# Graph attention on one core: VectorE multiplies two heads, not one, in six steps of 32 instead of two

## The chip, the core and the metric

The kernel runs on one core of a Trainium2 chip. Five engines work beside each other, each with its own queue of instructions: TensorE (PE, with its weight loads listed apart as PEld), VectorE (DVE), ScalarE (ACT), GpSimd (POOL) and SyncE (SP, which here only issues DMAs). They wait for one another through semaphores. The metric is the device time of one execution in microseconds; the time of the kernel before is the median of three runs.

## The reference

Two layers over 4096 nodes of 512 features, with one dense 4096 x 4096 matrix `adj` that is both the edge weight and the mask. Layer 0 is a single-head attention with `adj` added twice to the logits. The change touches layer 1 alone, a graph attention with 8 heads of 64 features:

```python
h = jnp.maximum(_layernorm(x, axis=-1), 0.0)
nX = (h @ W).reshape(n, NHEAD, OUT_DIM).transpose(1, 0, 2)
nX = a_ln * (nX - mean) / (std + EPS) + b_ln           # per head
at1 = jnp.einsum('kno,ok->kn', nX, a1)[:, :, None]
at2 = jnp.einsum('kno,ok->kn', nX, a2)[:, :, None]
kg = leaky_relu(at1 + at2.transpose(0, 2, 1), 0.2)     # head x node x node
kg = kg * graph[None]
mg = jnp.where(mask[None], kg, NEG_FILL)
attention = jax.nn.softmax(mg, axis=-1)
y = attention @ nX + nX
x = x + jax.nn.elu(y.transpose(1, 0, 2).reshape(n, 512))
```

So for each of 8 heads and each pair of nodes a logit is formed, multiplied by the edge weight, exponentiated and used as weight in a sum over nodes.

## The kernel before

`fast_path` does the work (a second path for extreme values is compiled in and is not run here). Layer 0 takes the first 2070 us or so. Layer 1 runs in 512 steps: 8 chunks of 512 target nodes, in each chunk 2 groups of 4 heads (`HG`), and in each of these 16 groups 32 steps over blocks of 128 source nodes (`NB` = 32). "Group k" below is the k-th of these 16, and "step m of a group" the step with number m modulo 32. One step handles a block of 128 sources x 512 targets for four heads; its results go through these functions:

- `z_sums(n+1)`, TensorE: into two PSUM tiles `d`, each holding two heads (`pair[0]`: heads 0 and 1, `pair[1]`: heads 2 and 3), it puts the sum of the two attention terms (L950) and then the mask, as a product of a bf16 tile with an identity (L955). There are three such buffers for the two tiles of a step. The order is heads 2, 3, 0, 1.
- `relu(n+1)`, ScalarE: for heads 0 and 1 a Relu into the SBUF tile `t` (L962). Six buffers of `t` exist.
- `leaky(n)`, VectorE: for heads 2 and 3 one `scalar_tensor_tensor` each (L972), then the product with the edge weights `g` for as many heads as VectorE has to take (`mine`, L977), then the addition of `pair[0]` to heads 0 and 1 of `t` (L978), which completes their leaky ReLU.
- `weigh(n)`, GpSimd: the product with `g` for the remaining heads, all of them in SBUF (L985).
- `exponent(n-3)`, ScalarE: the exponent of all four heads, 2048 columns (L988).
- `values(n-4)`, TensorE: the product with the features `nX`, accumulated over the 32 steps (L1001).

Each engine takes its instructions in the order in which the loop emits them: within iteration n of the loop `values(n-4)`, `exponent(n-3)`, `leaky(n)`, `weigh(n)`, `z_sums(n+1)`, `relu(n+1)`. So ScalarE takes the Relu of step n+1 only after the exponent of step n-3, and TensorE starts the sums of step n+1 only after the value products of step n-4.

At the end of a group `finish` spreads further work over the first steps of the next one: ScalarE copies the accumulators in step 3 (L1017), TensorE turns them back to rows in steps 4 and 5 (L1023), VectorE divides and adds in the same steps (L1032 to L1035), ScalarE does the passes of the ELU in steps 7 to 11 (L1045 to L1055), and GpSimd two additions of 1024 columns in steps 12 and 13 (L1059, L1063). Group 0 also carries the layer norm, projection and split of the last chunk's rows (`make_ready`, L258 to L408), and groups 1 to 4 each carry two GpSimd passes over 512 columns for those rows (L349, L350, in the fifth step).

How many heads VectorE multiplies is decided by the set `light`: in a step of the set VectorE takes two heads (3 and 2) and GpSimd two; in all other steps VectorE takes one and GpSimd three. Where VectorE takes two, the second L972 leaves its result in PSUM (`pair[1]`) instead of writing it to `t`.

Of the kernel before, what the change touches and what calls it, by code (L numbers as in the profile page):

```python
# [23 lines left out]
NB = N // P  # L24
# [22 lines left out]
@with_exitstack  # L47
def adj_preln_gnn_kernel(
    ctx: ExitStack,
    tc: tile.TileContext,  # L50
    x: bass.AP,
    adj: bass.AP,
    wqT: bass.AP,
    bq: bass.AP,
    wkT: bass.AP,
    bk: bass.AP,
    wvT: bass.AP,
    bv: bass.AP,
    w1: bass.AP,
    a1T: bass.AP,  # L60
    a2T: bass.AP,
    a_ln: bass.AP,
    b_ln: bass.AP,
    out: bass.AP,
):
    nc = tc.nc
    keep = ctx.enter_context(tc.tile_pool(name="keep", bufs=1))
    flag = keep.tile([1, 1], mybir.dt.int32, name="flag")
    fast_path(
        tc, flag, x, adj, wqT, bq, wkT, bk, wvT, bv, w1, a1T, a2T, a_ln, b_ln, out  # L70
    )

    low = nc.values_load(flag[0:1, 0:1])  # L73
    with tc.If(low > 0):
        general_path(tc, x, adj, wqT, bq, wkT, bk, wvT, bv, w1, a1T, a2T, a_ln, b_ln, out)
# [3 lines left out]
def fast_path(  # L79
# [796 lines left out]
    with tc.tile_pool(name="ga_in", bufs=2) as inputs, tc.tile_pool(  # L876
# [6 lines left out]
        n_steps = len(STEPS)  # L883
# [1 line left out]
        inverses = gat.tile([P, NI, 2, 2, 2, 4], F32, name="inverses")  # L885
        loads, logits, zs, groups = {}, {}, {}, {}

        light = {n + d for n in range(NB + 3, n_steps, NB) for d in (9, 10)}
        later = {}

        def load_adj(q):
# [684 lines left out]
```

## Time and profile before

| | us |
|---|---|
| median of 3 runs | 3968.43 (3968.31 to 3969.87) |
| profiled execution | 3965.98 |
| its span, first to last instruction | 3964.2 |
| layer 1: first product on GpSimd (L985) starts | 2092.1 |
| last product on GpSimd starts | 3937.3 |
| group 0 (start of one group's first L985 to the next's) | 157.0 |
| groups 1 to 4, each | 114.6 to 114.7 |
| groups 5 to 14, each | 112.1 to 112.2 |

A line of the timeline reads: start, duration (both in us), engine, line of the kernel, operation, what is written and read with its shape, how many instructions are merged in it, and in brackets the idle time of the engine before it with the instruction that ended this. A line of the groups reads: line, engine, operation, shapes, count, then busy us and mean ns of one, then the idle time before it and what ended most of it. Two instructions of VectorE can overlap a little at their ends in these records, so the distance from start to start says more of its pace than the sum of durations. A line of the windows gives the window, its length, and the busy us of each engine in it, then the granted clock of TensorE (1.00 is full), the DMA engines' busy share and GB/s.

### The profile page before, as it was taken

What the parts mean: (1) busy time and instruction counts of PE and PEld (TensorE: products, weight loads), DVE (VectorE), ACT (ScalarE), POOL (GpSimd) and SP (SyncE); (2) the same over time, 40 slices, a digit from 0 to 9 for tenths busy, and PEclk for the clock granted to TensorE, in tenths of its full rate; (3) what the DMA queues carried; (4) which work ended last, traced back from release to release, by engine and by line L of the source; (5) the groups of instructions that cost most, each with busy time, mean ns of one, the idle gap of its engine ahead of it and who ended that gap; (6) DMA issues with size and microseconds to landing.
All of it is one profiled execution on the core that took longest, in us unless ns stands there. A gap on an engine that the chain in (4) does not pass through costs nothing. (4 is left out here: it accounts for less than half of the span.)

```text
span 3964.2 us, 43905 instructions
## 1 busy us (share of the span) xinstructions
PE 3774.4 (95%) x15217; PEld 1789.4 (45%) x15370; DVE 2890.3 (73%) x4328; ACT 1797.0 (45%) x1581; POOL 2564.4 (65%) x1281
## 2 busy tenths in 40 slices
PE   8989999999999999999998899999999999999997
PEld 4446666666666666666653222222222222222222
DVE  5435556565565656556556799999999999999996
ACT  1001011111111111111115688888888888888887
POOL 3432225243242525234256999999999999999998
PEclk9999999999999999999998999999999999999999
DMA  6466656667675766757556544444444444444442
GB/s 208 175 206 193 201 179 204 200 194 211 184 220 161 222 182 191 214 186 222 166 153 189 145 138 146 146 142 142 134 143 144 139 145 146 146 140 146 132 150 79
DMA packets 554407, 670.37 MB, mean 169 GB/s; under 512 B 79808, under 2 KB 397504, under 8 KB 534720
## 3 DMA queue, kind: packets, MB, share of 16 engines
q1 hardware_dynamic: 552112, 665.70, 54.7%
q8 instruction: 122, 2.00, 0.2%
q10 hardware_dynamic: 2064, 1.77, 0.2%
q14 instruction: 109, 0.89, 0.1%
HBM read 495.12 MB, written 172.23 MB: 168 GB/s over the span
## 5 line engine op out<-in xcount | busy, mean ns | idle before, releaser
L985 POOL TENSOR_TENSOR t<-t,g 128x1536 f32<-128x1536 f32 (+1 forms) x512 | 1724.0, 3440 | 47.6 <-DVE t L978 26.9
L1001 PE MATMUL acc<-t,nX 128*64 128x512 f32 x4096 | 996.3, 607 | 72.1 <-ACT t L988 58.0
L737 POOL TENSOR_TENSOR total<-total,aT 128x512 f32<-128x512 f32 x248 | 340.5, 1373 | 1059.0 <-ACT aT L732 1051.9
L988 ACT ACTIVATE t<-t 128x2048 f32<-128x2048 f32 x512 | 975.8, 1906 | 87.7 <-POOL t L985 86.6
L747 PE MATMUL acc<-v,aT 128*128 128x512 f32 x2048 | 961.9, 593 | 0.0
L732 ACT ACTIVATE aT<-aT 128x512 f32<-128x512 f32 x256 | 161.3, 630 | 1323.2 <-DVE aT L727 1315.2
L962 ACT ACTIVATE t<-d 128x1024 f32<-128x1024 f32 x512 | 524.8, 1025 | 239.1 <-PE d L955 216.6
L978 DVE TENSOR_TENSOR t<-t,d 128x1024 f32<-128x1024 f32 x512 | 620.2, 1211 | 7.3 <-ACT t L962 7.3
L955 PE MATMUL d<-nb,ident_b 128*128 128x512 bf16 x1895 | 514.8, 385 | 14.9 <-issue 9.3
L1001 PEld LDWEIGHTS acc<-t,nX 128*64 128x64 f32 x4096 | 250.5, 136 | 597.6 <-issue 340.9
L747 PEld LDWEIGHTS acc<-v,aT 128*128 128x128 f32 x2048 | 389.9, 190 | 272.3 <-issue 244.8
L972 DVE SCALAR_TENSOR_TENSOR d<-u,at2m,d 128x512 f32<-128x512 f32 x542 | 407.3, 752 | 51.9 <-PE d L955 31.1
L727 DVE TENSOR_TENSOR aT<-aT,X 128x256 f32<-128x256 f32 x512 | 215.0, 420 | 279.6 <-PE X L719 276.3
L972 DVE SCALAR_TENSOR_TENSOR t<-u,at2m,d 128x512 f32<-128x512 f32 x482 | 360.0, 747 | 50.0 <-DVE d L972 0.9
L727 DVE TENSOR_TENSOR aT<-aT,Z 128x256 f32<-128x256 f32 x384 | 159.6, 416 | 290.5 <-PE Z L719 285.8
L977 DVE TENSOR_TENSOR t<-d,g 128x512 f32<-128x512 f32 (+1 forms) x512 | 366.3, 715 | 4.3 <-DMA g<-gT_d 1.4
L950 PE MATMUL d<-z,z 6*128 6x512 bf16 x2048 | 252.2, 386 | 45.5 <-DVE t L977 22.7
L711 DVE SCALAR_TENSOR_TENSOR gs<-ng,aT 128x512 f32<-128x512 bf16 x256 | 286.0, 1117 | 10.3 <-DMA gT_d<-gs 1.7
L950 PEld LDWEIGHTS <-z 6*128 6x128 bf16 x2048 | 76.8, 91 | 456.0 <-issue 451.9
L719 PE MATMUL Z<-qt,hS 128*128 128x256 f32 x1024 | 266.0, 383 | 8.6 <-DVE aT L727 8.4
L955 PEld LDWEIGHTS <-ident_b 128*128 128x128 bf16 x2048 | 159.2, 98 | 242.9 <-issue 123.4
L719 PE MATMUL X<-qt,hS 128*128 128x256 f32 x1024 | 263.9, 381 | 0.0
(161 smaller groups left out, 3120.6 us busy)
## 6 DMA issues: line engine op xcount, KB each, us to landing
g<-gT_d SPq DMA_DIRECT2D x128, 1024.0 KB, 5.5
ag<-in_adj_dram SPq DMA_DIRECT2D x256, 256.0 KB, 5.2
hT<-h_d SPq DMA_DIRECT2D x64, 1024.0 KB, 5.9
hS<-s_d SPq DMA_DIRECT2D x64, 1024.0 KB, 8.2
gT_d<-gs SPq DMA_DIRECT2D x256, 256.0 KB, 2.7
nb<-nT_d SPq DMA_DIRECT2D x128, 512.0 KB, 5.3
nT_d<-ng SPq DMA_DIRECT2D x256, 128.0 KB, 3.1
z<-z_d SPq DMA_DIRECT2D x143, 128.0 KB, 4.7
```

Source lines behind the costliest of these rows:

```text
L719: seq(nc.tensor.matmul(out, a, b, start=start and k == 0, stop=k == 1, skip_group_check=not start,))
L727: seq(nc.vector.tensor_add(p, p, part))
L737: seq(nc.gpsimd.tensor_add(totals[ic], totals[ic], p))
L747: seq(nc.tensor.matmul(sums[ic][b], probs[s][:, ts(b, P)], v[:, jt, :], start=jt == 0, stop=jt == NB - 1))
L955: seq(nc.tensor.matmul(pair[hh // 2][:, hh % 2, :], ident_b, ng[:, jt % JB, :], start=False, stop=True))
L962: seq(nc.scalar.activation(t[:, 0:2, :], zs[n][0], AF.Relu, scale=4.0))
L972: seq(nc.vector.scalar_tensor_tensor(pair[1][:, e, :] if e > 1 - mine else t[:, 2, :], u4[:, e, :], at2m[:, jt, h : h + 1], pair[1][:, e, ...
L977: seq(nc.vector.tensor_mul(t[:, HG - mine : HG, :], pair[1][:, 2 - mine : 2, :], g))
L978: seq(nc.vector.tensor_add(t[:, 0:2, :], t[:, 0:2, :], pair[0]))
L985: seq(nc.gpsimd.tensor_mul(t[:, 0:mine, :], t[:, 0:mine, :], g))
L988: seq(nc.scalar.activation(logits[n], logits[n], AF.Exp))
L1001: seq(nc.tensor.matmul(grp["acc"][hf][ts(e, HD), :], nX[jt // SB][:, jt % SB, hg * HG + 2 * hf + e, :], t[:, 2 * hf + e, :], start=jt == 0 ...
```

## The change

The set `light` is replaced. Before, it held two steps in each of groups 1 to 15: steps 12 and 13, those in which GpSimd also has its two additions for the group before. Now it holds steps 1, 8, 12, 13, 19 and 25 of every group, group 0 included. Nothing else is edited, and no instruction changes its place in its queue; the shapes and operands of L972, L977 and L985 in the steps concerned follow from the set. (One blank line is added too, so in the changed kernel the lines below it have numbers higher by one.)

```diff
-        light = {n + d for n in range(NB + 3, n_steps, NB) for d in (9, 10)}
+
+        light = {n for n in range(n_steps) if n % NB in (1, 8, 12, 13, 19, 25)}
         later = {}
```

Where the set is used (unchanged):

```python
def leaky(n):
    ...
    mine = 2 if n in light else 1
    for e in (1, 0):
        h = hg * HG + 2 + e
        seq(nc.vector.scalar_tensor_tensor(
            pair[1][:, e, :] if e > 1 - mine else t[:, 2, :], u4[:, e, :],
            at2m[:, jt, h : h + 1], pair[1][:, e, :], ALU.max, ALU.add,
        ))
    g = loads[n // JB][0][:, jt % JB, :].unsqueeze(1).to_broadcast([P, mine, GC])
    seq(nc.vector.tensor_mul(t[:, HG - mine : HG, :], pair[1][:, 2 - mine : 2, :], g))
    seq(nc.vector.tensor_add(t[:, 0:2, :], t[:, 0:2, :], pair[0]))

def weigh(n):
    mine = 2 if n in light else 3
    g = loads[n // JB][0][:, STEPS[n][2] % JB, :].unsqueeze(1).to_broadcast([P, mine, GC])
    t = logits[n]
    seq(nc.gpsimd.tensor_mul(t[:, 0:mine, :], t[:, 0:mine, :], g))
```

## The prediction

> **What bounds the kernel now.** I read the page first (busy shares), then the busy time per window, the groups by line with shapes kept apart, the waits, and last the timeline of VectorE, because the change moves work between two engines that are both nearly full. The page, and the windows of three whole groups of 32 steps in layer 1:
>
> ```profile
> PE 3774.4 (95%) x15217; PEld 1789.4 (45%) x15370; DVE 2890.3 (73%) x4328; ACT 1797.0 (45%) x1581; POOL 2564.4 (65%) x1281
> ...
> 2363.72:2478.47 114.75, 106.50 (x523) 31.66 (x528) 106.92 (x135) 96.44 (x72) 114.67 (x38) 1.00 0.45 141
> 2707.71:2819.83 112.12, 106.09 (x520) 32.24 (x528) 105.97 (x135) 95.78 (x72) 112.12 (x35) 1.00 0.44 142
> 2819.83:2931.94 112.11, 106.22 (x521) 32.27 (x528) 106.00 (x135) 95.83 (x72) 112.11 (x35) 1.00 0.45 142
> ```
>
> The windows' columns after the length are PE, weight loads, DVE, ACT, POOL. From about 2090 us on, one group lasts 112.1 us (114.7 in groups 1 to 4) and GpSimd is busy for all of it: it sets the pace. VectorE shows 106, but this understates it, as the gap it needs between two instructions is not busy time. Its timeline, in the first group that GpSimd does not hold back, and the last step of layer 1:
>
> ```profile
> 2243.12 1.21 DVE L978 TENSOR_TENSOR t<-t,d 128x1024 f32<-128x1024 f32 x1
> ...
> 2286.26 1.22 DVE L978 TENSOR_TENSOR t<-t,d 128x1024 f32<-128x1024 f32 x1 [0.27 <-ACT t L962]
> 2288.20 1.55 DVE L972 SCALAR_TENSOR_TENSOR d<-u,at2m,d 128x512 f32<-128x512 f32 x2 [0.73 <-PE d L955]
> 2289.84 1.23 DVE L977 TENSOR_TENSOR t<-d,g 128x1024 f32<-128x1024 f32 x1
> 2290.99 1.21 DVE L978 TENSOR_TENSOR t<-t,d 128x1024 f32<-128x1024 f32 x1
> 2292.11 1.54 DVE L972 SCALAR_TENSOR_TENSOR d<-u,at2m,d 128x512 f32<-128x512 f32 x2
> 2293.76 1.23 DVE L977 TENSOR_TENSOR t<-d,g 128x1024 f32<-128x1024 f32 x1
> 2294.90 1.21 DVE L978 TENSOR_TENSOR t<-t,d 128x1024 f32<-128x1024 f32 x1
> 2296.03 0.75 DVE L972 SCALAR_TENSOR_TENSOR d<-u,at2m,d 128x512 f32<-128x512 f32 x1
> ...
> 2299.28 0.75 DVE L972 SCALAR_TENSOR_TENSOR d<-u,at2m,d 128x512 f32<-128x512 f32 x1
> ...
> 2353.67 1.21 DVE L978 TENSOR_TENSOR t<-t,d 128x1024 f32<-128x1024 f32 x1
> ...
> 3930.70 1.21 DVE L978 TENSOR_TENSOR t<-t,d 128x1024 f32<-128x1024 f32 x1
> ```
>
> A step with one head on VectorE takes 2299.28 - 2296.03 = 3.25 us from start to start, with no wait in it; a step with two ("light", because it is light for GpSimd) takes 2296.03 - 2292.11 = 3.92 us. The whole group from 2243.12 to 2353.67 takes 110.55 us; its last two steps were already held by GpSimd (0.14 and 0.18 us over 3.25), so VectorE alone needs 110.2 us for a group with two light steps. GpSimd's 112.1 stands only 1.9 us over it. That margin decides the case.
>
> GpSimd's own prices, by shape, and the order of a group around its two light steps:
>
> ```profile
> L985 POOL TENSOR_TENSOR t<-t,g 128x1536 f32<-128x1536 f32 x481 | 1649.3, 3504 | 27.0 <-DVE t L978 26.9
> L985 POOL TENSOR_TENSOR t<-t,g 128x1024 f32<-128x1024 f32 x30 | 72.4, 2412 | 0.0
> ...
> 2863.26 2.43 POOL L1059 TENSOR_TENSOR e<-e,y 128x1024 f32<-128x1024 f32 x1
> 2865.57 2.45 POOL L985 TENSOR_TENSOR t<-t,g 128x1024 f32<-128x1024 f32 x1
> 2867.90 2.46 POOL L1063 TENSOR_TENSOR e<-e,xi 128x1024 f32<-128x1024 f32 x1
> 2870.24 65.26 POOL L985 TENSOR_TENSOR t<-t,g 128x1536 f32<-128x1536 f32 x19
> ```
>
> From start to start a product of three heads costs 65.26/19 = 3.43 us, one of two heads or an ELU addition about 2.33 us: 30 x 3.43 + 4 x 2.33 = 112.2 us, the measured group. In groups 1 to 4 the two passes for the last chunk's own rows (L349, L350) add 2.55 us.
>
> [...] The rows of L977 show 1225 and 684[...] the trace has 3504 - 2412 = 1092 ns. So a head costs GpSimd about twice what it costs VectorE, and moving one looks like a bargain. [...] the light steps at 2288 to 2296 run with GpSimd busy and keep their prices. [...] VectorE has little time to give.
>
> **The change part by part.** The set goes from two light steps in each of groups 1 to 15 (12 and 13 modulo 32: 30 steps) to six in each of the 16 groups (1, 8, 12, 13, 19, 25: 96 steps). No queue is reordered and no DMA moves; in each of the 66 further steps L985 shrinks to 1024 columns, L977 grows to 1024, and the second result of L972 stays in PSUM.
>
> GpSimd: four more light steps a group save 4 x (3.43 - 2.33) = 4.4, so 107.8 us (110.3 in groups 1 to 4).
>
> VectorE: four more light steps add 4 x (3.92 - 3.25) = 2.7, so 112.9 us at most. The bound changes hands: GpSimd now idles about 5 us a group, which costs nothing, and absorbs the 2.55 us of groups 1 to 4.
>
> Can VectorE follow its own sum? In the group above its waits beyond the plain prices are 0.5 us before the reciprocal of step 4, and 0.2, 0.36 and 0.8 us in steps 10 to 12, where ScalarE's extra passes for ELU (steps 7 to 11) make its exponents late, PE's value products wait for those, and the sums of the next step come late. Step 8, now light, gives ScalarE and PE 0.67 us just before. Following the instructions: the 0.2 of step 10 goes (PE waited 0.24 us for the exponent there), but the two Relu passes and the Exp that make steps 11 and 12 late start about 0.5 us later too, so most of that stays. I take 0.15 us off: 112.75. Bounds: nothing comes off (112.9), or all 0.67 (112.2). For the other added steps I find no cover: steps 1, 19 and 25 lie where VectorE runs back to back.
>
> How long were the 15 groups before, by VectorE's own clock? (3930.70 - 2243.12)/15 = 112.5 us; the 114.7 of groups 1 to 4 and the 112.1 of the rest, less the ground VectorE had to give up at first. So 15 x (112.75 - 112.5) = +3.8 us.
>
> The end: GpSimd now trails VectorE by 5.44 us at the last step (VectorE's last addition ends at 3931.9, GpSimd's last product starts at 3937.3), and the tail hangs on GpSimd. With VectorE as pacer the backlog is built afresh in each group: from nothing at step 12, +0.74 at 13 (2.33 + 2.33 - 3.92), +1.4 at 14, +0.18 in each plain step, and -0.48 and then -0.9 around each of steps 19 and 25, which leaves about 1.8 at step 31. That gives -3.6 us.
>
> Group 0 (2092 to 2249 us) has no light step now and gets six. Steps 8 and 12 are hidden: VectorE then waits more than 3 us for the projection's matmuls anyway (L301 waits on PE). Step 25 is on the path, step 1 and 13 too (the next sums wait for L977). Step 19 adds 0.67 on VectorE but takes 1.1 from GpSimd ahead of the scalars' split, which PE waits for. Between +1.2 and +2.7; I take +2.0.
>
> Sum: +3.8 - 3.6 + 2.0 = +2.2 us. The profiled execution took 3965.98 us (span 3964.2 and 1.8 around it), so it would take 3968.2; the median shown is 3968.43, 2.5 above, and I carry the difference to it: 3970.6, say 3970.5.
>
> **Rivals.**
> 1. ScalarE's lateness in steps 10 to 12 dissolves, with VectorE and GpSimd no longer entangled. Then 1.37 us of wait go in each group: 110.2 + 2.7 - 1.37 = 111.5, 15 x (111.5 - 112.5) - 3.6 + 2.0 = -17, or 3952 us. For it: step 8 is light just there. Against: the same waits stand, to 0.01 us, in groups where GpSimd's backlog differs by 2.6 us, so they do not come from GpSimd but from ScalarE's own sum, which is the same after.
> 2. Slower, by one mechanism: PE has almost no slack. A plain PE round takes about 3.24 us against VectorE's 3.25, and half of the next step's sums cannot start before L977 has released its PSUM pair. L977 is 0.55 us longer in a light step, so the first L972 after each added light step may wait, as it waits 0.54 us in step 1 at 2092 us where PE's clock is low. 60 added steps x 0.54 = 32 us, 4002 us. Against: after both light steps at 2288 and 2292 L972 starts with no wait. It decides from (7.9 - 2.2)/60 = 0.1 us per added step.
> 3. GpSimd's saving arrives whole (15 x 4.4 = 66 us, 3902): would need VectorE at 107.8 a group, which its own 110.2 with only two light steps excludes. No chance given.
>
> **How the numbers follow.** A measurement of this kernel tells about 0.2% (7.9 us) from no change. My forecast, that the pace passes to VectorE at nearly the same value, has 0.77: its bounds (15 x -0.55 and 15 x +0.15, and 0.2 us of unforeseen wait a group upward, the group 0 spread) give 3961 to 3977, nearly all within 0.2%; of it 0.70 no change, 0.06 slower, 0.01 faster. Rival 1 has 0.09 (0.08 faster, 0.01 no change), rival 2 0.14, all slower, with smaller waits likelier than the full one. Faster 0.09, no change 0.71, slower 0.20. The range 3961 to 3980 leaves out rival 1 and most of rival 2.
>
> **What would show it.** GpSimd's busy time in a group window falls to about 108 of about 112.7, with idle before L985 released by L978; VectorE's step is 3.92 in six places and 3.25 elsewhere; groups 1 to 4 become 2 us shorter and the later ones 0.6 us longer. L972 idle on PE after plain light steps would show rival 2; no waits at steps 10 to 12, rival 1. A group under 111.5 or over 113.3 us would make the forecast wrong.

## The result, and the profile after

| | before | after |
|---|---|---|
| median of 12 runs | 3968.26 us (3965.82 to 3970.69) | 3968.94 us (3965.39 to 3971.58) |
| after / before | | 1.0002 (95%: 0.9994 to 1.0009) |
| profiled span | 3964.2 us | 3968.8 us |
| of it from the start of the first L985 (L986 after) to the end | 1872.07 us | 1871.95 us |

The change moves the time by nothing that can be measured. The 4.6 us between the two profiled spans lie ahead of GpSimd's first product of layer 1, where nothing was changed: it starts at 2092.1 us in one execution and at 2096.9 in the other. From there to the end the two need the same.

That is a sum of parts that cancel, not a change without effect. First the busy time of the engines on the page after, then three whole groups of 32 steps (groups 2, 5 and 6; after the length: PE, weight loads, DVE, ACT, POOL), then GpSimd's waits from group 1 on (who waits, for whom, us, times, longest). All line numbers after are higher by one.

```profile
PE 3810.7 (96%) x15370; PEld 1800.1 (45%) x15370; DVE 2918.1 (74%) x4328; ACT 1783.0 (45%) x1581; POOL 2495.9 (63%) x1281
```

```profile
2361.27:2474.28 113.01, 108.57 (x531) 33.08 (x530) 107.73 (x135) 94.71 (x73) 110.37 (x37) 1.00 0.46 143
2699.88:2812.53 112.65, 108.56 (x530) 33.06 (x528) 107.72 (x135) 94.98 (x73) 108.01 (x35) 1.00 0.45 142
2812.53:2925.18 112.65, 108.56 (x530) 33.06 (x528) 107.72 (x135) 94.98 (x73) 107.97 (x35) 1.00 0.45 142
```

```profile
POOL t L986 <- DVE t L979: 62.0, 67, 1.4
```

GpSimd's 112.1 us of work a group have become 108.0, and the 4.6 that it lacks to 112.65 are idle time, ended by VectorE's last instruction of a step (62 us in all, 4.1 a group, in the line above). Before, GpSimd waited for nothing from group 1 on. VectorE is the pacer now, although its 107.7 busy us are 96% of the window. The busy share does not tell it: the engine that sets the pace is busy for 107.7 us of a group, and one with 4.6 us to spare for 108.0. A reader has to go to the timeline. VectorE's, around a light step away from all waits (step 19 of group 6):

```profile
2880.83 1.21 DVE L979 TENSOR_TENSOR t<-t,d 128x1024 f32<-128x1024 f32 x1
2881.96 1.54 DVE L973 SCALAR_TENSOR_TENSOR d<-u,at2m,d 128x512 f32<-128x512 f32 x2
2883.60 1.23 DVE L978 TENSOR_TENSOR t<-d,g 128x1024 f32<-128x1024 f32 x1
2884.74 1.21 DVE L979 TENSOR_TENSOR t<-t,d 128x1024 f32<-128x1024 f32 x1
2885.87 0.75 DVE L973 SCALAR_TENSOR_TENSOR d<-u,at2m,d 128x512 f32<-128x512 f32 x1
2886.73 0.75 DVE L973 SCALAR_TENSOR_TENSOR t<-u,at2m,d 128x512 f32<-128x512 f32 x1
2887.39 0.68 DVE L978 TENSOR_TENSOR t<-d,g 128x512 f32<-128x512 f32 x1
2887.99 1.21 DVE L979 TENSOR_TENSOR t<-t,d 128x1024 f32<-128x1024 f32 x1
```

The light step takes 2885.87 - 2881.96 = 3.91 us, and the step behind it has no idle time in brackets: each instruction follows the one before at the usual distance, 0.1 us behind the end of an L973 that leaves its result in PSUM (`d`), and 0.08 or 0.09 us before the end of any other. There are 38 such L973 in a group, so some 3.8 us: most of the 4.9 that the busy sum leaves out.

The rest of the sum reads off VectorE's last addition of group 0 and of group 15, and off GpSimd's last product, after and before:

```profile
2248.12 1.21 DVE L979 TENSOR_TENSOR t<-t,d 128x1024 f32<-128x1024 f32 x1
...
3938.93 1.21 DVE L979 TENSOR_TENSOR t<-t,d 128x1024 f32<-128x1024 f32 x1
```

```profile
3941.90 3.50 POOL L986 TENSOR_TENSOR t<-t,g 128x1536 f32<-128x1536 f32 x1
...
3937.33 3.49 POOL L985 TENSOR_TENSOR t<-t,g 128x1536 f32<-128x1536 f32 x1
```

(3938.93 - 2248.12)/15 = 112.72 us a group, against 112.51 before: +3.2 us over 15 groups. GpSimd's last product starts 2.97 us behind the start of VectorE's last addition (6.63 before), and from that addition to the end of the span it takes 29.87 us instead of 33.49: -3.6. Group 0, from the start of the first product on GpSimd to the end of VectorE's last addition, took 152.5 us against 152.2: +0.3. Together -0.1 us.

### The profile page after: what moved, and what is told of

Its sections match the earlier page's. It is cut to its first block, busy times and chain, and to the rows that moved or that the text cites. A ratio compares the mean times of both kernels' runs of the same rounds, so it can differ in the third digit from the quotient of the medians.

```text
span 3968.8 us, 44058 instructions
## 1 busy us (share of the span) xinstructions
PE 3810.7 (96%) x15370; PEld 1800.1 (45%) x15370; DVE 2918.1 (74%) x4328; ACT 1783.0 (45%) x1581; POOL 2495.9 (63%) x1281
## 5 line engine op out<-in xcount | busy, mean ns | idle before, releaser
L986 POOL TENSOR_TENSOR t<-t,g 128x1536 f32<-128x1536 f32 (+1 forms) x512 | 1654.2, 3263 | 117.1 <-DVE t L979 94.9
L956 PE MATMUL d<-nb,ident_b 128*128 128x512 bf16 x2048 | 536.8, 385 | 1.7 <-DMA nb<-nT_d 1.7
L973 DVE SCALAR_TENSOR_TENSOR d<-u,at2m,d 128x512 f32<-128x512 f32 x608 | 456.0, 750 | 38.8 <-PE d L956 33.2
L978 DVE TENSOR_TENSOR t<-d,g 128x512 f32<-128x512 f32 (+1 forms) x512 | 401.8, 785 | 12.0 <-DMA g<-gT_d 2.2
L951 PE MATMUL d<-z,z 6*128 6x512 bf16 x2048 | 283.3, 384 | 69.7 <-DVE t L978 47.1
L973 DVE SCALAR_TENSOR_TENSOR t<-u,at2m,d 128x512 f32<-128x512 f32 x416 | 310.7, 747 | 43.2 <-DVE d L973 0.9
L951 PEld LDWEIGHTS <-z 6*128 6x128 bf16 x2048 | 89.8, 91 | 498.2 <-issue 494.0
```

Of the source, the lines that this page charges most:

```text
L951: seq(nc.tensor.matmul(pair[hh // 2][:, hh % 2, :], z2[rows, ts(jt % JB, P)], groups[ic, hg]["z1"][rows, :], start=True, stop=False,))
L956: seq(nc.tensor.matmul(pair[hh // 2][:, hh % 2, :], ident_b, ng[:, jt % JB, :], start=False, stop=True))
L973: seq(nc.vector.scalar_tensor_tensor(pair[1][:, e, :] if e > 1 - mine else t[:, 2, :], u4[:, e, :], at2m[:, jt, h : h + 1], pair[1][:, e, ...
L978: seq(nc.vector.tensor_mul(t[:, HG - mine : HG, :], pair[1][:, 2 - mine : 2, :], g))
L986: seq(nc.gpsimd.tensor_mul(t[:, 0:mine, :], t[:, 0:mine, :], g))
```

## The experiments

Every experiment was judged by its time and by two distances in its trace: how long a group takes, from one last addition of VectorE to the next group's, and how long group 0 takes.

**1. Step 19 of group 0 alone**

```diff
+        light = ... | {19}      # on top of the set of before
```

> The kernel before with one more light step, step 19 of group 0; nothing else. Theory (that step takes 1.1 us from GpSimd ahead of the split of the scalars, which PE waits for, and this outweighs VectorE's 0.67 us): from the first L985 to the last L978 of group 0, 152.2 us before, it falls to 151.3 to 151.8. Rival (step 19 costs VectorE's 0.67 us, and what made group 0 cheap in the changed kernel lies in steps 1, 8, 12 or 13): 152.7 to 152.9. The whole time moves by under 1 us either way.

Measured: group 0 took 151.4 us, inside the first theory's window; 3967.75 us in one run. Alone it settles nothing, because one and the same group 0 differs by up to 1.8 us between executions (151.1 to 152.9 with the changed kernel's six steps). All of this spread lies in step 4, in step 5 and in steps 21 to 24, none of them a light step. Without step 5 and steps 21 to 24, group 0 takes 116.8 us in the three executions in which VectorE has no light step there, 117.4 in the three with step 19 alone, and 118.8 in three of the four with six (in experiment 3 it takes 118.2, as step 4 was 0.6 us shorter). So what VectorE pays can be read in spite of the spread: 0.66 us for step 19, 2.0 for all six.

**2. GpSimd relieved, VectorE not burdened**

This kernel leaves out work: in the added light steps nobody multiplies head 2 by its edge weights.

```diff
+        light = {n for n in range(n_steps) if n % NB in (1, 8, 12, 13, 19, 25)}
+        both = {n + d for n in range(NB + 3, n_steps, NB) for d in (9, 10)}
 ...
-            mine = 2 if n in light else 1     # in leaky: VectorE
+            mine = 2 if n in both else 1
```

> GpSimd is relieved as in the change (two heads in the six steps), but VectorE multiplies one head in the four added ones, as before: head 2 stays without its edge weights there, so that product is left out. Theory (the pace passes to VectorE, whose own sum is 110.2 us a group plus 2.65 for the added steps in the changed kernel): without the added product each later group takes 110.2 to 110.4 us, 15 groups some 33 us less than before, 3932 to 3937 us in all. Rival (GpSimd still sets the pace in the changed kernel): 107.8 us a group, 3900 us or less. Rival (PE is what holds the changed kernel at 112.65): no gain over the changed kernel, 3968.

Measured: 3931.12 us (ratio 0.9908, 0.9892 to 0.9925), a little under the window, groups of 110.2 us. Two whole groups:

```profile
2798.01:2908.23 110.22, 107.34 (x530) 32.95 (x528) 105.19 (x136) 94.96 (x73) 107.96 (x35) 1.00 0.45 145
2908.23:3018.45 110.22, 107.33 (x530) 32.97 (x528) 105.20 (x135) 94.94 (x73) 107.96 (x35) 1.00 0.45 144
```

GpSimd has the same 108 us of work as in the changed kernel, and still idles 2.3 us: VectorE's own sum with two light steps, 110.2, is the floor, as the prediction read it from group 1. PE, with the same work, fits into 110.2 us too, so it does not hold the changed kernel at 112.65. What the four products of head 2 cost on VectorE is 112.65 - 110.22 = 2.43 us a group (four times 0.66, less the 0.2 of step 10 that only the changed kernel saves), 36 us over 15 groups, about what the change would have gained without it.

**3. Nearly half of GpSimd's saving given back as useless work**

```diff
+            if n >= NB and n % NB in (19, 25):
+                seq(nc.gpsimd.tensor_mul(idle, g[:, 0, :], g[:, 1, :]))
```

> The changed kernel, with a product of 512 columns into an unused tile given to GpSimd in steps 19 and 25 of groups 1 to 15: 2 x 1.27 us more work a group, which gives GpSimd back more than half of the 4.4 us that the change took from it. Theory (GpSimd idles some 5 us a group in the changed kernel and is not on the path): groups 5 to 15 stay at 112.65 us, groups 1 to 4 at 112.65 to 113.2, the time within 3 us of the changed kernel. Rival (GpSimd still sets the pace): 2.5 us more a group, 38 us in all, 4007.

Measured: 3970.39 us (1.0007, 0.9999 to 1.0016), 1.5 us over the changed kernel and inside the first theory's window; the groups stay at 112.65 (113.0 in three of them, as in the changed kernel itself).

```profile
2811.09:2923.75 112.66, 108.56 (x530) 33.05 (x528) 107.72 (x135) 94.97 (x73) 109.95 (x37) 1.00 0.44 142
```

GpSimd works 2.0 us more a group than in the changed kernel and the group does not notice. What moves is the end: GpSimd's last product starts 4.97 us behind VectorE's last addition instead of 2.97. Experiments 2 and 3 together settle who paces the changed kernel.

**4. The passes of the ELU spread out**

In the changed kernel steps 11 and 12 of VectorE still last 0.34 and 0.8 us longer than their work (3.59 and 4.71 us from last addition to last addition, where 3.25 and 3.91 are usual). I held ScalarE's crowded passes of steps 7 to 11 for the cause.

```diff
-                (4, "end", room), (4, "end", lambda: minus(0)), (5, "end", lambda: minus(1)),
-                (6, "end", lambda: exps(0)), (6, "end", positive), (7, "end", lambda: exps(1)),
-                (8, "end", less_one),
-                (9, "end", elu), (10, "end", close),
+                (4, "end", room), (4, "end", lambda: minus(0)), (6, "end", lambda: minus(1)),
+                (8, "end", lambda: exps(0)), (10, "end", lambda: exps(1)),
+                (12, "end", lambda: positive(0)), (14, "end", lambda: positive(1)),
+                (16, "end", lambda: less_one(0)), (18, "end", lambda: less_one(1)),
+                (20, "end", elu), (21, "end", close),
 ...
-            if n < n_steps and STEPS[n][2] == 12:     # load_rows
+            if n < n_steps and STEPS[n][2] == 26:
```

(`positive` and `less_one` are split into halves too, and the loop runs 11 iterations longer so that the last pieces are issued.)

> The changed kernel, with ScalarE's passes of the ELU spread over steps 7 to 21 in pieces of 512 columns, one in every second step, and GpSimd's two additions moved behind them to steps 23 and 24. Theory (VectorE paces, and the 0.34 and 0.8 us that it waits in steps 11 and 12 come from ScalarE's late exponents): these waits go, each group takes 111.4 to 111.6 us instead of 112.65, and the time falls by 15 to 18 us to 3951 to 3954. Rival (the waits come from PE having no slack in light steps, not from ScalarE): they stay in steps 12 and 13 and the time stays at 3969.

Measured: 3969.24 us (1.0003, 0.9995 to 1.0012), 112.60 us in most groups. The theory fell. Its rival was right on the time and not on the place: 0.2 us is left in step 12, and steps 16, 18, 22 and 24 now take 3.46 to 3.48 us. So five of the eight pieces are each followed, three steps later, by a wait of about 0.2 us. The other three would show it in steps 10, 14 and 20. These come one or two steps behind a light step (8, 13 and 19), and there is no wait in them. ScalarE, PE and VectorE around step 16 of group 8:

```profile
3091.54 0.62 ACT L1049 ACTIVATE e<-e 128x512 f32<-128x512 f32 x1
3092.06 1.90 ACT L988 ACTIVATE t<-t 128x2048 f32<-128x2048 f32 x1
```

```profile
3094.01 1.94 PE L1001 MATMUL acc<-t,nX 128*64 128x512 f32 x8 [0.24 <-ACT t L988]
3095.88 0.40 PE L950 MATMUL d<-z,z 6*128 6x512 bf16 x4
...
3097.18 1.94 PE L1001 MATMUL acc<-t,nX 128*64 128x512 f32 x8
```

```profile
3095.52 1.21 DVE L978 TENSOR_TENSOR t<-t,d 128x1024 f32<-128x1024 f32 x1
3096.86 0.76 DVE L972 SCALAR_TENSOR_TENSOR d<-u,at2m,d 128x512 f32<-128x512 f32 x1
```

The pass stands behind the Relu and ahead of the exponent, so the exponent starts 0.52 us late. The value products wait for it (0.24 us in brackets), the sums behind them in PE's queue come as much later, and L972 starts 1.34 us after L978 where 1.13 is usual. PE's round, 3.17 us from 3094.01 to 3097.18 with no wait in it, is nearly as long as VectorE's 3.25, so little can be caught up in plain steps; behind a light step, which takes VectorE 3.91 us, there is room, and that fits the three places without a wait. It is the delay of one exponent that counts, not ScalarE's sum.

**5. The same pieces, ahead of the Relu**

```diff
-                (4, "end", room), (4, "end", lambda: minus(0)), (6, "end", lambda: minus(1)),
+                (4, "mid", room), (4, "mid", lambda: minus(0)), (6, "mid", lambda: minus(1)),
 ...
```

and so for all eight pieces; "mid" lies between the exponent and the next Relu.

> As the kernel before it in this list of experiments (six light steps, ScalarE's passes of the ELU in pieces of 512 columns in every second step from 7 to 21), but each piece stands right after the exponent in ScalarE's queue, ahead of the next Relu, and no longer behind the Relu and ahead of the next exponent. New theory (spreading failed because a pass ahead of the exponent delays the exponent by 0.52 us, the value products wait for it, and PE, whose round is as long as VectorE's, hands on what is over some 0.3 us; ahead of the Relu there are 0.4 us of idle ScalarE and 0.6 us before VectorE needs the Relu): no wait of VectorE is left in steps 11 to 24, a group takes 111.3 to 111.6 us, and the time is 3950 to 3955. Rival (each pass costs VectorE 0.2 us wherever it stands, as PSUM or ScalarE's sum is short): 112.6 us a group, 3969. Rival (a late Relu delays the addition on VectorE instead): waits before L978 of 0.1 us or more a piece, 112.2 or more a group.

Measured: 3956.1 us (0.9974, 0.9963 to 0.9985), groups of 111.5 to 112.1, mostly 111.7 to 111.8: a little over both windows, and clearly not the rivals'. Around the same step ScalarE now shows the following.

```profile
3084.82 1.90 ACT L988 ACTIVATE t<-t 128x2048 f32<-128x2048 f32 x1
3086.62 0.62 ACT L1052 ACTIVATE y<-y 128x512 f32<-128x512 f32 x1
3087.14 1.02 ACT L962 ACTIVATE t<-d 128x1024 f32<-128x1024 f32 x1
3088.06 1.90 ACT L988 ACTIVATE t<-t 128x2048 f32<-128x2048 f32 x1
3090.39 1.03 ACT L962 ACTIVATE t<-d 128x1024 f32<-128x1024 f32 x1 [0.42 <-PE d L955]
```

The piece fills the idle time that ScalarE has before a Relu (0.42 in the last line), and the next exponent starts 3.24 us after the one before, on time. Steps 12 to 24 take 3.25 and 3.91 us. What is left over 111.5 is a wait in steps 4 and 5: GpSimd's two additions, now in steps 23 and 24, drive its backlog (from the end of VectorE's last addition of a step to the start of GpSimd's product) to 5 us, and VectorE runs into it. In step 0 of group 8 it still stands at 5.2 us; in experiments 4 and 7, with 4.7 and 3.2 us there, steps 4 and 5 show no such wait.

**6. The same with the two light steps of before**

```diff
-        light = {n for n in range(n_steps) if n % NB in (1, 8, 12, 13, 19, 25)}
+        light = {n + d for n in range(NB + 3, n_steps, NB) for d in (9, 10)}
```

> The same order of ScalarE's passes, with the two light steps of the kernel before. Theory (with two light steps GpSimd sets the pace, so that VectorE's waits cost nothing): groups 5 to 14 stay at 112.1 us and groups 1 to 4 at 114.65, the time within 4 us of before. Rival (those waits cost time in the kernel before as well): 1.1 us less a group, 3951.

Measured: 3972.45 us (1.0014, 1.0006 to 1.0023), 112.5 us in the later groups. Freeing VectorE gained nothing here, where GpSimd paces, as held; but it even cost 5 us, outside the first theory's 4, which I had not expected. GpSimd's waits name them (from group 1 on):

```profile
POOL t L985 <- DVE t L978: 5.4, 12, 0.8
```

The two light steps stood where the two additions were. With the additions gone from there GpSimd runs dry before its product of step 14, some 0.45 us in each of twelve groups; these 5.4 us are about what the time grew by.

**7. Four light steps, with the pieces ahead of the Relu**

```diff
+        light = {n for n in range(NB, n_steps) if n % NB in (15, 23, 24, 28)}
+        light |= {19} | {n for n in range(NB, 5 * NB) if n % NB == 8}
```

> The same order of ScalarE's passes with four light steps (15, 23, 24 and 28) in groups 5 to 15, five (8 too) in groups 1 to 4, and only step 19 in group 0. Theory (VectorE's sum without the waits is 110.2 - 1.4 + 2 x 0.67 = 110.2 us a group, GpSimd's 112.2 - 2 x 1.1 = 110.0): groups 5 to 14 take 110.2 to 110.6 us, groups 1 to 4 111.0 to 111.7, and the time is 3932 to 3938. Rival (two engines that are both full hand their waits to each other): 111.2 us or more a group, 3950 or more.

Measured: 3933.06 us (0.9911, 0.9897 to 0.9924), groups of 110.15 to 110.5 from 5 on and 110.8 to 111.1 in 1 to 4; the time is inside the theory's window. This is the version that beats both kernels, by 34 and 36 us, and it leaves nothing out. Groups 2 and 8:

```profile
2356.21:2467.02 110.81, 107.05 (x521) 33.22 (x528) 106.82 (x136) 94.67 (x75) 110.73 (x37) 1.00 0.47 145
3020.19:3130.71 110.52, 107.17 (x521) 33.23 (x528) 106.20 (x136) 94.78 (x75) 110.52 (x35) 1.00 0.47 146
```

GpSimd is busy throughout again, and VectorE waits from group 1 to the last step for PE's rows after each group and hardly for anything else:

```profile
DVE inverses L1033 <- PE pt L1024: 6.2, 15, 0.5
DVE t L973 <- DVE d L973: 1.4, 3, 0.5
```

The new order of the passes alone is experiment 6. The four light steps with the passes in their old places were not run, so how much of the 34 us they would bring without that order is not shown.

**8. Three light steps, nothing else**

```diff
+        light = {n for n in range(NB, n_steps) if n % NB in (8, 12, 13)}
+        light |= {19} | {n for n in range(NB, 5 * NB) if n % NB == 25}
```

> The kernel before with another set alone: three light steps (8, 12 and 13) in groups 5 to 15, four (25 too) in groups 1 to 4, step 19 in group 0. Theory (GpSimd needs 112.2 - 1.1 = 111.1 us, VectorE 110.2 + 0.67 - 0.15 = 110.7): groups 5 to 14 take 111.1 to 111.3 us, groups 1 to 4 112.5 to 112.7, and the time is 3947 to 3953. Rival (the pace cannot be split between the two, and any further light step costs VectorE's price): 112.7 us a group, 3970.

Measured: 3956.66 us (0.9973, 0.9964 to 0.9982): 10 us faster, but over the theory's window, as the groups take 111.9 us, 0.8 more than GpSimd's sum and 1.2 more than VectorE's. GpSimd in group 7 shows where:

```profile
2923.23 40.03 POOL L986 TENSOR_TENSOR t<-t,g 128x1536 f32<-128x1536 f32 x12
2964.06 2.38 POOL L986 TENSOR_TENSOR t<-t,g 128x1024 f32<-128x1024 f32 x1 [0.80 <-DVE t L979]
```

It waits 0.80 us in step 12, where its backlog has run out, and earlier in the same group, in steps 0 to 5, VectorE waits because the backlog stands at 5.5 us in steps 0 to 3, where it has stopped growing, as it does at 5.4 in the kernel before. The sums fit; the order within the group does not.

## Why the prediction was right, step by step

The forecast was 3970.5 us, 2.1 over the kernel before; measured are 3968.94, 0.7 over it. That the sum is near nothing is not luck: the two large terms that cancel were each right to 0.6 us. What was wrong lies in group 0 and in a reason.

- **GpSimd falls to 107.8 us a group and idles.** Shown: 108.0 busy, 62 us of idle from group 1 on, and 2 us of added work that nobody notices (experiment 3).
- **VectorE sets the pace at 112.75.** It is 112.65 in twelve of fifteen groups and in the mean 112.72. The prices were right to 0.01 us: 3.91 in a light step, 3.25 in a plain one. By the rows of the kernel before, a head costs VectorE 1225 - 684 = 541 ns (L977, 1024 and 512 columns), half of GpSimd's 1092. The floor of 110.2 with two light steps is shown by experiment 2.
- **Of VectorE's waits in steps 10 to 12, 0.15 us go.** The 0.2 of step 10 went, the 0.36 and 0.8 of steps 11 and 12 stayed (0.34 and 0.8). The reason given was only half right. That these waits come from ScalarE's passes is so; that ScalarE's sum is too long there is not: spreading the same passes removed none of the time (experiment 4), placing them ahead of the Relu removed most (experiment 5). So rival 1 did not come true: of its 1.37 us a group, 1.14 stayed.
- **15 groups +3.8 us, the end -3.6.** Measured +3.2 and -3.6.
- **Group 0 +2.0, between 1.2 and 2.7.** Measured +0.3 in the profiled pair. This term was mis-sized. Steps 1, 19 and 25 took 0.66 us longer each, while step 13, charged 0.67, cost nothing: steps 12 to 14 took 16.47 us together after 16.42, since step 14 shrank from 4.47 to 3.85. That is +2.0 on VectorE. What was too small is the other side: step 5 and steps 21 to 24 took 33.7 us after 35.4. In the other executions they took 32.9 to 34.7 where GpSimd's product of step 19 is the small one, and 35.2 where it is not (experiment 6). So the saving that the prediction named for step 19 does seem to arrive, and larger. How large stays open, as these steps also go with the clock: in all ten traces TensorE is granted 0.50 at the start of layer 1, until 10.9 to 18.0 us after GpSimd's first product, and step 5 took 7.6 us where this ended first and 9.8 to 9.9 in the three where it ended last.
- **Rival 2**, a wait for PE behind every added light step, did not appear: no idle before L973 in the step after one from group 1 on (in group 0 it is 0.48 us in step 2 and 0.54 in step 20, the same as before). The tightness of PE that it rested on is real, and experiment 4, with a round of 3.17 us for PE against VectorE's 3.25, shows what it does, but the sums behind a light step come in time.

## What to carry to other kernels

When two engines share a loop, a piece of work moved from the fuller one gains at most the distance to the second one's own sum, the moved work included (here from 112.51 us a group in the mean to 112.65, so nothing); read that sum from start to start, in a stretch where the first engine does not hold it back (here 110.2 us, where busy time said 106). Once they are level, the next gain lies in the waits of the new pacer and in where the work stands within the loop: the same two engines gave 0, 10 and 34 us with three arrangements. What a short pass on a third engine costs here depends on what stands behind it in the queue: 0.62 us of ScalarE ahead of an exponent made that 0.52 us late and left the group at 112.60 us (experiment 4), the same piece ahead of the Relu, where ScalarE idles 0.42 us without it, at 111.7 to 111.8 (experiment 5). So it goes where that engine idles anyway, not ahead of an instruction that a full engine waits for.

## What was unexpected of the hardware

In some groups one step of VectorE lasts 0.35 us longer, with no other engine named: in the changed kernel step 8 of group 2, step 29 of group 9 and step 21 of group 10. One such place, in experiment 7:

```profile
3061.86 0.75 DVE L973 SCALAR_TENSOR_TENSOR t<-u,at2m,d 128x512 f32<-128x512 f32 x1 [0.46 <-DVE d L973]
```

The gap between two L973 is 0.46 us instead of 0.1. In the changed kernel it costs some 1 us in all (three groups of 113.0).

The place belongs to the program and not to the time. Step 29 of group 9 and step 21 of group 10 are late in all six kernels in which ScalarE's passes stand as before; in the four with the pieces it is step 27 of group 6 and step 11 of group 8 instead. And in each of the 25 gaps of this kind in the ten traces, a packet of q14, one of the two DMA queues that the profile lists as "instruction", starts within 2 us behind the late instruction (0.7 us in the three of the changed kernel), though only 43 packets of that queue fall between 2250 and 3935 us there. Whether the two are linked, and how, is not shown: no run here tests it.
